# Four-layer graph network on one core: score, attention, adjacency and quantile products queued behind each step's column-tile block

## The chip, the core and the metric

The kernel runs on one core of a Trainium2 chip. The metric is the time of one execution on the device in microseconds (us); the median of the runs shown is compared. A core has engines that run side by side and wait for each other through semaphores: TensorE (PE, matrix products into PSUM; its weight loads are listed apart as PEld), VectorE (DVE), ScalarE (ACT), GpSimd (POOL, idle here) and SyncE (SP, which issues the transfers). Each engine takes its instructions in a fixed order.

## The reference, cut to what matters

`x` is 16 graphs of 1024 nodes with 64 features, `adj` their 0/1 adjacency. Four layers follow each other, each `x = x + f(relu(layernorm(x)), adj)`:

```
layer 0: thin out neighbours by rank (dilation); per node and feature take the 0.25, 0.5 and
         0.75 quantiles over the neighbours, weighted 0.25, 0.5, 0.25; add h; two-layer MLP; mask
layer 1: (adj + I) @ h / rowsum(adj + I)
layer 2: 8 heads: s = exp(gamma0) * q.k/8 + exp(gamma1) * adj; softmax(s) @ v; projection
layer 3: adj @ (h @ W) + bias
```

Layer 0 is the costly one: six order statistics (three quantiles, each between two neighbours in the sorted list) for 1024 nodes, 64 features and 16 graphs ("elements").

## The kernel before, in words

**Two streams.** `picks()` (L760) is layer 0. It makes 16 x 8 x 2 x 6 = 1536 *steps*, 96 an element: element `b`, group `g` of 8 features, half `t` of the nodes (512 columns), order statistic `q`. `layers()` (L1287) is all the rest: it turns every adjacency matrix (`turned`, L1076, during element 0) and then, for an element whose layer 0 is done, runs layers 1, 2 and 3. So layers of element `b` run beside the steps of element `b+1`, and those of the last one run alone after the last step (`alone`). The driver (L1295 to L1299) traces both by due times: a step yields .42, and pieces of layers are traced until their own yields have used that up. The 40.3 units of layers of an element just fill 96 steps.

**A step.** `compare(n)` (L794) makes on DVE three 128x2048 passes: `le` (L800), `wa` (L802), `wb` (L804), in four rotating buffers (`a4`). PE then multiplies them by small stationary matrices 32 columns wide: the *column block*, 16 products at L823, four each of `prep<-wb` and `prep<-wa` and eight of `val<-le`. Each uses one of four column tiles of the 128x128 array (`tile_position`). ACT copies `prep` to `wi` (L830) and `val` to `vs`. One step later `bits` (L835) makes `bit` on DVE and `pz` on PE (L843); two steps later `value` (L846) makes `vs` on DVE (L850), and after a group's sixth statistic the *quantile sums* `agg` (L856, PE, again 32 columns wide, two instructions for each float32 product), which DVE weighs (`w`, L867) in a later step. `prep`, `val` and `pz` share two PSUM buffers (tag `pa`).

Besides, each step advances `group` (L694), which prepares the tables of the step six later: per feature pair a product over the neighbours (`whole`, L716), then `remainder` (L728), `differences` (L737) and `low_part` (L743), all 128x128 on PE, with ACT passes between them; and `background`, the sorting and thinning of the next element, mostly on DVE.

**Layer 2** (L1113) goes through four pairs of heads, and for each through eight chunks of 128 rows (`i`, L1195). A chunk loads its row `ad` (SP, ACT scales it), and for each head `e` makes the *scores* `sp` (L1213: 64 rows of the array, 1024 columns, one PSUM buffer of its own). DVE adds `ad` and takes the minimum (L1226); ACT takes the exponential with a sum (L1235); PE turns the result in eight pieces (`pcols`, L434) that ACT copies to `eT` (L437; two buffers, tag `bt`). The *attention sum* `ao` (L1240) is 32 instructions of 64 columns, one half of the array a head; then ACT's copy `aoT`, the projection `pp` (L1249) and ACT's copy `att`. `residual` (L1135) adds four chunks at a time to `xr` on DVE.

**Layers 1 and 3** use the *adjacency sum* `two` (`weighted`, L1060, L1064): 16 instructions of 64 columns.

**The order of the work.** A scheduler places the instructions of each engine before the run, by readiness in its own model of time, and by priority, which is the order of tracing. `adjoining` (L383) holds a group of PE products together: all but the first are queued behind the first (`issue_after`: an order of issue, no wait for its end) and get high priority. The first stands where the scheduler puts it. It is used for every block named above.

Of the kernel before, what the change touches and what calls it, by code (L numbers as in the profile page):

```python
# [8 lines left out]
F32 = mybir.dt.float32  # L9
# [12 lines left out]
P = 128  # L22
# [3 lines left out]
NQ = 6  # L26
# [12 lines left out]
def tile_preln_adj_stack(  # L39
# [30 lines left out]
    nc = tc.nc  # L70
# [38 lines left out]
    def b4(name, shape=(P, N), dt=F32):  # L109
        return a4(name, shape, dt) if alone else sb.tile(list(shape), dt, tag="b4", bufs=2, name=name)  # L110
# [6 lines left out]
    def small(name, shape, dt=F32, bufs=3):  # L117
        return sb.tile(list(shape), dt, tag="s_" + name, bufs=bufs, name=name)
# [264 lines left out]
    def adjoining(made):  # L383

        first = next(made)
        with tc.issue_after(first.ins), tc.high_priority():
            for _ in made:
                pass


    def norm_relu(xr, h, t2):
# [368 lines left out]
    def picks():  # L760
# [33 lines left out]
        def compare(n):  # L794
            b, g, t, q = steps[n]
            el = els[b]
            hs = slice(t * 512, (t + 1) * 512)
            cum, c1, c0 = tables[b, g, t]
            le = a4("le", (P, 4, 512), HP)
            nc.vector.tensor_tensor(le, cum, bc(el.krow[q][:, None, hs], [P, 4, 512]), OP.is_lt)  # L800
            wa = a4("wa", (P, 4, 512), HP)
            nc.vector.tensor_tensor(wa, le, c0, OP.mult)  # L802
# [13 lines left out]
            nc.tensor.matmul(  # L816
                prep, sel_q[:, q, :], el.kq[:, hs], start=True, stop=False, skip_group_check=True
            )

            def made():  # L820
                for i, (dst, w, r) in enumerate(rounds):
                    for pp in range(4):
                        yield nc.tensor.matmul(  # L823
                            dst[32 * pp : 32 * pp + 32, :], w[pp], r[pp], start=i == 2, stop=i in (1, 3),
                            tile_position=(0, 32 * pp), skip_group_check=True,
                        )

            adjoining(made())
            wi = a2("wi")
            nc.scalar.copy(wi, prep)  # L830
            vs = sb.tile([P, 512], F32, tag="v", bufs=7, name="vs")
            act(vs, val, AF.Copy, scale=1.0 / UP)
            state[n] = [wi, vs]
# [12 lines left out]
        def value(n):  # L846
            b, g, t, q = steps[n]
            el = els[b]
            pz, vs = state.pop(n)
            nc.vector.scalar_tensor_tensor(vs, pz, 80.0, vs, op0=OP.is_equal, op1=OP.mult)  # L850
            vs_of[q] = vs
            if q < NQ - 1:
                return
            agg = pb("agg")
            adjoining(
                nc.tensor.matmul(  # L856
                    agg[32 * (q_ % 4) : 32 * (q_ % 4) + 32, :], sel_t[:, q_ // 4, :], vs_of[q_],
                    start=q_ < 4, stop=q_ > 1, tile_position=(0, 32 * (q_ % 4)),
                    skip_group_check=True,
                )  # L860
                for q_ in range(NQ)
            )
            def weigh(behind):
                hs = slice(t * 512, (t + 1) * 512)
                w = a2("w")
                with tc.issue_after(behind.ins) if behind else ExitStack():
                    nc.vector.tensor_tensor(w, agg, el.coef[:, hs], OP.mult)  # L867
# [192 lines left out]
    def weighted(aT, h):  # L1060

        two = pb("two", (P, P))
        adjoining(
            nc.tensor.matmul(  # L1064
                two[j % 2 * D : j % 2 * D + D, :], h[:, j, :], aT[:, j, :], start=j < 2,
                stop=j >= C - 2, tile_position=(0, j % 2 * D), skip_group_check=True,
            )
            for j in range(C)
        )
        part = small("aoT", [P, P], bufs=2)  # L1070
        nc.scalar.copy(part, two)
        po = pb("po", (P, D))
        nc.tensor.matmul(po, part, ident2, start=True, stop=True)
        return po
# [38 lines left out]
    def layer2(b, xr):  # L1113
# [19 lines left out]
        for pr in range(H // 2):  # L1133
# [50 lines left out]
            for t in range(NH):  # L1184
# [6 lines left out]
                    )  # L1191
                nc.scalar.copy(v[:, 4 * t : 4 * t + 4, :], pv)
            yield 0.5
            for i in range(C):
                if i == C // 2:  # L1195
                    qT = queries(1, False)
                if i % (C // 2) == 0:
                    att = sb.tile([P, C // 2, 2, D], F32, tag="att", bufs=1, name="att")
                    sums = small("sums", [P, C // 2, 2], bufs=2)
                ad = adj_rows(b, i)  # L1200
                act(ad, ad, AF.Copy, scale=gm[:, i, 1:2])
                eTs = []
                ss = [b4("s") for _ in range(2)]
                nms = [None, None]
                cols = slice(i % 4 * P, (i % 4 + 1) * P)
                for e in range(2):
                    if alone and e:
                        sps = [pc_("sp") for _ in range(NH)]
                    else:
                        sp = ps.tile([P, NH, 512], F32, tag="sp", bufs=1, name="sp")  # L1210
                        sps = [sp[:, t, :] for t in range(NH)]
                    adjoining(
                        nc.tensor.matmul(  # L1213
                            sps[t], qT[t * D : (t + 1) * D, t ^ e, cols],
                            kT[t * D : (t + 1) * D, e, :], start=True, stop=True,
                        )
                        for t in range(NH)
                    )
                    if alone and e:
                        parts = [(sps[t], slice(t * 512, (t + 1) * 512)) for t in range(NH)]  # L1220
                    else:
                        parts = [(sp.rearrange("p t k -> p (t k)"), slice(0, N))]
                    for s, hs in parts:

                        nm = small("nm", [P, 1], bufs=6)
                        nc.vector.tensor_tensor_reduce(  # L1226
                            ss[e][:, hs], s, ad[:, hs], -1.0, nms[e] if hs.start else 3.0e38,
                            op0=OP.add, op1=OP.min, accum_out=nm,
                        )
                        nms[e] = nm  # L1230
                while late:
                    residual(*late.pop())
                yield 0.4
                for e in range(2):
                    act(ss[e], ss[e], AF.Exp, bias=nms[e], scale=-1.0, accum_out=sums[:, i % (C // 2), e : e + 1])  # L1235
                    eTs.append(chunk_cols(ss[e], "eT"))
                yield 0.3
                ao = pb("ao", (P, P))
                adjoining(
                    nc.tensor.matmul(  # L1240
                        ao[e * D : (e + 1) * D, :], v[:, j, e * D : (e + 1) * D], eTs[e][:, j, :],
                        start=j == 0, stop=j == C - 1, tile_position=(0, e * D), skip_group_check=True,
                    )
                    for j in range(C) for e in range(2)
                )
                aT = small("aoT", [P, P], bufs=2)
                nc.scalar.copy(aT, ao)
                pp = pb("pp", (P, 2, D))
                nc.tensor.matmul(pp, aT, wproj[:, pr], start=True, stop=True)  # L1249
                nc.scalar.copy(att[:, i % (C // 2)], pp)  # L1250
                if (i + 1) % (C // 2) == 0:
                    late.append((i + 1 - C // 2, att, sums))
                yield 0.3
        residual(*late.pop())

    def layer3(b, xr):
# [80 lines left out]
```

## Time and profile before

| what | us |
|---|---|
| median of 3 runs (lowest, highest) | 12469.6 (12461.9, 12470.75) |
| the profiled execution's own time | 12481.28 |
| its span, first to last instruction | 12479.1 |
| PE busy | 11308.4 (91%) |
| DVE busy | 11269.9 (90%) |
| ACT busy | 10053.6 (81%) |
| first comparison (L800) to the last | 318 to 12053 |
| a middle element (96 steps) | 735 to 758 |
| alone after the last step | 421 |

A line of instruction groups reads: line, engine, operation, what it writes `<-` what it reads, rows*columns of the array for PE, shapes, count | busy time, mean ns of one | idle time of the engine just before them, and what ended it. Ends of PE's instructions are modelled, starts are not: lengths on PE are read from one start to the next. A line of waits reads: who waited `<-` for whom: us in all, times, longest. In a timeline, like instructions in a row are merged (x8), with the engine's idle time before them in brackets.

### The profile page before, as it was taken

The page shows a single profiled execution, that of the slowest core. Times are in us where ns is not written, and L with a number is a line of the kernel's source. Part 1 is how long each engine was busy: PE and PEld are TensorE (multiplying, and loading weights), DVE is VectorE, ACT ScalarE, POOL GpSimd, SP SyncE. Part 2 cuts the span into 40 slices and gives each one's busy share as a digit, 9 for nine tenths or more (in the row PEclk, how much of TensorE's full clock was granted, in tenths as well). Part 3 has the DMA queues.
Part 4 walks back from the last instruction along what each step waited for, and adds up shares of the span by engine and source line. Part 5 has one row for each costly group of instructions (what it writes and reads, how often), then busy time and mean ns, then how long its engine had stood idle before and what let it go on. Part 6 is the DMA issues. An engine that isn't in the chain of part 4 may idle for free. (4 is left out here: it accounts for less than half of the span.)

```text
span 12479.1 us, 216279 instructions
## 1 busy us (share of the span) xinstructions
PE 11308.4 (91%) x85697; PEld 5374.3 (43%) x85697; DVE 11269.9 (90%) x17026; ACT 10053.6 (81%) x17672; POOL 3.3 (0%) x22
## 2 busy tenths in 40 slices
PE   3889989999899998999999998999989999999988
PEld 2334444444444444444444444444444444444445
DVE  8999989899898989989899998999989999887862
ACT  4988878888787887878788887888878888888866
POOL 0000000000000000000000000000000000000000
PEclk6999999999999999999999999999999999999988
DMA  7641121211212122121211212122121212211011
GB/s 238 232 142 56 53 76 59 77 60 54 72 55 80 59 63 65 54 82 57 71 59 60 75 56 74 55 70 68 56 72 55 83 55 60 78 32 56 30 53 57
DMA packets 520552, 908.01 MB, mean 73 GB/s; under 512 B 239728, under 2 KB 274672, under 8 KB 519536
## 3 DMA queue, kind: packets, MB, share of 16 engines
q1 hardware_dynamic: 519536, 894.18, 22.6%
q8 instruction: 672, 11.01, 0.4%
q14 instruction: 344, 2.82, 0.1%
HBM read 683.25 MB, written 206.57 MB: 71 GB/s over the span
## 5 line engine op out<-in xcount | busy, mean ns | idle before, releaser
L802 DVE TENSOR_TENSOR wa<-le,c 128x2048 f16<-128x2048 f16 x1536 | 1871.6, 1218 | 211.1 <-PE prep L823 169.4
L716 PE MATMUL px<-valid,cw 128*128 128x512 fp8e4 x8192 | 1955.5, 380 | 2.0 <-ACT cw L381 2.0
L804 DVE TENSOR_TENSOR wb<-le,c 128x2048 f16<-128x2048 f16 x1536 | 1871.3, 1218 | 0.0
L800 DVE TENSOR_TENSOR le<-cum,krow 128x2048 f16<-128x2048 int16 x1536 | 1868.6, 1217 | 0.6 <-ACT cum L381 0.6
L381 ACT ACTIVATE c<-px,shifts 128x512 f16<-128x512 f32 x2048 | 1432.4, 702 | 153.4 <-PE px L737 82.0
L1226 DVE CUSTOM_DVE_ANT_0 s<-sp,ad 128x1024 f32<-128x1024 f32 (+1 forms) x1024 | 1230.4, 1202 | 332.9 <-PE sp L1213 329.6
L381 ACT ACTIVATE s<-s,nm 128x1024 f32<-128x1024 f32 x1024 | 1189.5, 1162 | 293.7 <-DVE nm L1226 291.4
L716 PEld LDWEIGHTS <-cw 128*128 128x128 f16 x8192 | 800.8, 98 | 1074.2 <-issue 164.4
L1213 PE MATMUL sp<-kT,qT 64*128 64x512 f32 x4096 | 1220.8, 641 | 24.0 <-DVE nm L1226 22.7
L434 PE MATMUL pcols<-identf,s 128*128 128x128 f32 x8192 | 1153.0, 279 | 96.0 <-ACT s L381 48.5
L437 ACT COPY eT<-pcols 128x512 f32<-128x512 f32 x2048 | 1133.8, 605 | 57.9 <-PE pcols L434 54.6
L434 PEld LDWEIGHTS pcols<-identf,s 128*128 128x128 f32 x8192 | 907.6, 141 | 582.0 <-ACT eT L437 212.1
L830 ACT COPY wi<-prep 128x512 f32<-128x512 f32 x1536 | 919.5, 599 | 289.0 <-PE prep L823 266.8
L850 DVE SCALAR_TENSOR_TENSOR vs<-pz,vs 128x512 f32<-128x512 f32 x1536 | 1051.2, 684 | 86.9 <-PE pz L843 83.1
L1240 PE MATMUL ao<-eT,v 128*64 128x128 f32 x16384 | 1080.8, 279 | 28.3 <-ACT eT L437 25.3
L823 PE MATMUL val<-le,tab 128*32 128x512 f16 x12288 | 1063.6, 388 | 29.0 <-DVE vs L850 17.7
L1240 PEld LDWEIGHTS ao<-eT,v 128*64 128x64 f32 x16384 | 918.5, 138 | 289.7 <-ACT eT L437 154.5
L381 ACT ACTIVATE high<-px,shifts 128x512 f16<-128x512 f32 x1024 | 709.2, 693 | 378.6 <-PE px L716 375.3
L381 ACT ACTIVATE vs<-val 128x512 f32<-128x512 f32 x1536 | 953.1, 620 | 56.9 <-PE agg L856 32.5
L838 DVE TENSOR_SCALAR bit<-wi,to 128x512 int32<-128x512 int32 x1536 | 830.8, 541 | 3.8 <-ACT cw L381 2.8
L823 PE MATMUL prep<-wb,sel_w 128*32 128x512 f16 x6144 | 639.2, 395 | 194.6 <-DVE wb L804 191.0
L843 PE MATMUL pz<-bit,nth 128*128 128x512 bf16 x1536 | 615.3, 401 | 192.5 <-DVE bit L838 144.8
(264 smaller groups left out, 18128.8 us busy)
## 6 DMA issues: line engine op xcount, KB each, us to landing
ad<-in_adj_dram SPq DMA_DIRECT2D x768, 512.0 KB
aT<-adjT SPq DMA_DIRECT2D x256, 512.0 KB
adjT<-aT SPq DMA_DIRECT2D x128, 512.0 KB
md<-sm SPq DMA_DIRECT2D x216, 256.0 KB
sb<-md SPq DMA_DIRECT2D x216, 256.0 KB
rem_d<-rem SPq DMA_DIRECT2D x128, 256.0 KB
left_d<-nb SPq DMA_DIRECT2D x128, 256.0 KB
lr<-left_d SPq DMA_DIRECT2D x256, 128.0 KB
```

The source lines that it names most:

```text
L381: nc.scalar.activation(out_, in_, func, **kw)
L434: nc.tensor.transpose(pt[:, c, :], ad[:, (4 * s + c) * P : (4 * s + c + 1) * P], identf)
L437: nc.scalar.copy(aT[:, 4 * s : 4 * s + 4, :], pt)
L716: yield nc.tensor.matmul(px[pp], w[:, j, :], valid[:, j, :], start=False, stop=j == C - 1, skip_group_check=True,)
L800: nc.vector.tensor_tensor(le, cum, bc(el.krow[q][:, None, hs], [P, 4, 512]), OP.is_lt)
L802: nc.vector.tensor_tensor(wa, le, c0, OP.mult)
L804: last = nc.vector.tensor_tensor(wb, le, c1, OP.mult)
L823: yield nc.tensor.matmul(dst[32 * pp : 32 * pp + 32, :], w[pp], r[pp], start=i == 2, stop=i in (1, 3), tile_position=(0, 32 * pp), skip_gr ...
L850: nc.vector.scalar_tensor_tensor(vs, pz, 80.0, vs, op0=OP.is_equal, op1=OP.mult)
L1213: nc.tensor.matmul(sps[t], qT[t * D : (t + 1) * D, t ^ e, cols], kT[t * D : (t + 1) * D, e, :], start=True, stop=True,)
L1226: nc.vector.tensor_tensor_reduce(ss[e][:, hs], s, ad[:, hs], -1.0, nms[e] if hs.start else 3.0e38, op0=OP.add, op1=OP.min, accum_out=nm,)
L1240: nc.tensor.matmul(ao[e * D : (e + 1) * D, :], v[:, j, e * D : (e + 1) * D], eTs[e][:, j, :], start=j == 0, stop=j == C - 1, tile_position ...
```

## The change

`adjoining` returns its last product. A new helper `following` makes a block like `adjoining`, but queues the whole block, its first product too, on PE behind the last product of the *leader*, with priority moved 1000 instructions ahead; its own last product is the next leader. `compare` sets the leader anew at each column block. `following` is used for `agg`, `two`, `sp` and `ao`; in the stretch after the last step (`alone`) it queues nothing.

`agg` and `ao` make their products in the reverse order, so that the first one needs the data that come last. In layer 2 the two heads' scores of a chunk are a step apart (a yield of 0.42 between them), the exponentials and turns have yields of 0.29 each, and `ao` with all that follows it (now `gathered`) is traced an iteration later, behind the second head's scores of the next chunk; the yields of a chunk still add up to 1.0.

```diff
@@ adjoining
         first = next(made)
+        last = first
         with tc.issue_after(first.ins), tc.high_priority():
-            for _ in made:
+            for last in made:
                 pass
+        return last
+
+    leader = []
+
+    def following(made):
+        with ExitStack() as behind:
+            if leader and not alone:
+                behind.enter_context(tc.issue_after(leader[0].ins))
+                behind.enter_context(tc.high_priority(1000))
+            leader[:] = [adjoining(made)]
@@ compare
-            adjoining(made())
+            leader[:] = [adjoining(made())]
@@ value
-            adjoining(
+            following(
...
-                    start=q_ < 4, stop=q_ > 1, tile_position=(0, 32 * (q_ % 4)),
+                    start=q_ > 1, stop=q_ < 4, tile_position=(0, 32 * (q_ % 4)),
...
-                for q_ in range(NQ)
+                for q_ in range(NQ - 1, -1, -1)
@@ weighted
-        adjoining(
+        following(
@@ layer2
+            def gathered(i, eTs, att, sums):
+                ao = pb("ao", (P, P))
+                following(
+                    nc.tensor.matmul(
+                        ao[e * D : (e + 1) * D, :], v[:, j, e * D : (e + 1) * D], eTs[e][:, j, :],
+                        start=j == C - 1, stop=j == 0, tile_position=(0, e * D), skip_group_check=True,
+                    )
+                    for j in range(C - 1, -1, -1) for e in (1, 0)
+                )
+                aT = small("aoT", [P, P], bufs=2)
+                nc.scalar.copy(aT, ao)
+                pp = pb("pp", (P, 2, D))
+                nc.tensor.matmul(pp, aT, wproj[:, pr], start=True, stop=True)
+                nc.scalar.copy(att[:, i % (C // 2)], pp)
+                if (i + 1) % (C // 2) == 0:
+                    late.append((i + 1 - C // 2, att, sums))
+
+            ready = []
             for i in range(C):
...
                 for e in range(2):
+                    s_, nm_ = b4("s"), None
...
-                    adjoining(
+                    following(
...
+                    ss.append((s_, nm_))
+                    if e == 0:
+                        yield 0.42
                 while late:
                     residual(*late.pop())
-                yield 0.4
-                for e in range(2):
-                    act(ss[e], ss[e], AF.Exp, bias=nms[e], scale=-1.0, accum_out=sums[:, i % (C // 2), e : e + 1])
-                    eTs.append(chunk_cols(ss[e], "eT"))
-                yield 0.3
...
-                yield 0.3
+                while ready:
+                    gathered(*ready.pop())
...
+                for e, (s_, nm_) in enumerate(ss):
+                    act(s_, s_, AF.Exp, bias=nm_, scale=-1.0, accum_out=sums[:, i % (C // 2), e : e + 1])
+                    eTs.append(chunk_cols(s_, "eT"))
+                    yield 0.29
+                ready.append((i, eTs, att, sums))
+            gathered(*ready.pop())
         residual(*late.pop())
```

More of the change, by code (lines that the diff above doesn't have):

```diff
@@ L1196, in layer2 @@
                     qT = queries(1, False)
-                if i % (C // 2) == 0:
-                    att = sb.tile([P, C // 2, 2, D], F32, tag="att", bufs=1, name="att")
-                    sums = small("sums", [P, C // 2, 2], bufs=2)
                 ad = adj_rows(b, i)
                 act(ad, ad, AF.Copy, scale=gm[:, i, 1:2])
-                eTs = []
-                ss = [b4("s") for _ in range(2)]
-                nms = [None, None]
+                eTs, ss = [], []
                 cols = slice(i % 4 * P, (i % 4 + 1) * P)
                 for e in range(2):
+                    s_, nm_ = b4("s"), None
                     if alone and e:
@@ L1226, in layer2 @@
                         nc.vector.tensor_tensor_reduce(
-                            ss[e][:, hs], s, ad[:, hs], -1.0, nms[e] if hs.start else 3.0e38,
+                            s_[:, hs], s, ad[:, hs], -1.0, nm_ if hs.start else 3.0e38,
                             op0=OP.add, op1=OP.min, accum_out=nm,
                         )
-                        nms[e] = nm
+                        nm_ = nm
+                    ss.append((s_, nm_))
+                    if e == 0:
+                        yield 0.42
                 while late:
                     residual(*late.pop())
-                yield 0.4
-                for e in range(2):
-                    act(ss[e], ss[e], AF.Exp, bias=nms[e], scale=-1.0, accum_out=sums[:, i % (C // 2), e : e + 1])
-                    eTs.append(chunk_cols(ss[e], "eT"))
-                yield 0.3
[L1238 to L1252, printed above, removed]
-                yield 0.3
+                while ready:
+                    gathered(*ready.pop())
+                if i % (C // 2) == 0:
+                    att = sb.tile([P, C // 2, 2, D], F32, tag="att", bufs=1, name="att")
+                    sums = small("sums", [P, C // 2, 2], bufs=2)
+                for e, (s_, nm_) in enumerate(ss):
[4 more added lines that the diff above has]
+            gathered(*ready.pop())
         residual(*late.pop())
```

## The prediction

> **What bounds the kernel now.** I read four views in this order: the page's busy shares, busy time by stage, the list of waits, and the timeline of TensorE. The page first:
>
> ```profile
> PE 11308.4 (91%) x85697; PEld 5374.3 (43%) x85697; DVE 11269.9 (90%) x17026; ACT 10053.6 (81%) x17672; POOL 3.3 (0%) x22
> ```
>
> TensorE (PE) and VectorE (DVE) are both about nine tenths busy, so an average names no bound. By stage (columns: stretch, its length, then busy time and count of PE, PEld, DVE, ACT, POOL): two middle elements, the last two, and the rest after the last step.
>
> ```profile
> 2442.00:3183.00 741.00, 690.13 (x5301) 325.01 (x5304) 686.06 (x1066) 609.57 (x1072) 0.00 (x0) 0.98 0.21 64
> 3183.00:3941.00 758.00, 697.89 (x5298) 328.64 (x5294) 715.75 (x1046) 613.09 (x1075) 0.00 (x0) 0.98 0.21 65
> ...
> 10647.00:12058.00 1411.00, 1332.80 (x10402) 626.38 (x10400) 1176.51 (x1573) 1169.12 (x2070) 0.00 (x0) 0.99 0.15 48
> 12058.00:12479.00 421.00, 338.79 (x2486) 224.05 (x2486) 125.10 (x280) 230.50 (x445) 0.00 (x0) 0.85 0.18 58
> ```
>
> In a middle element each engine idles 42 to 60 us of 741 or 758: they take turns at being late. In the last two elements there is less background work for DVE, it idles 234 us, and PE only 78: there PE is the bound. Over the ten middle elements (2442 to 9912 us) the same view adds up to 548 us of idle PE and 463 us of idle DVE. What ends DVE's idle time there (who waits, for whom, total us, times, longest):
>
> ```profile
> DVE s L1226 <- PE sp L1213: 101.1, 58, 3.9
> DVE wa L802 <- PE prep L823: 75.9, 85, 2.4
> DVE o L1055 <- PE y L1051: 74.6, 10, 8.0
> DVE w L867 <- PE agg L856: 58.5, 15, 6.0
> DVE vs L850 <- PE pz L843: 30.9, 30, 2.6
> DVE gm L1122 <- PE pg L1120: 23.7, 10, 3.8
> ```
>
> These six are 365 of the 463 us: what DVE waits for last is PE, in four fifths of its idle time. So time taken off PE shortens the run as long as such waits are left, up to some 36 us an element. ACT, at 610 of 750, waits for both.
>
> **What a change of tile size costs on PE.** The timeline of PE alone (start, length, instruction; only starts can be trusted):
>
> ```profile
> 6004.77 0.38 PE L737 MATMUL px<-high,dif 128*128 128x512 f16 x1
> 6004.98 0.38 PE L737 MATMUL px<-low,dif 128*128 128x512 f16 x1
> 6005.29 1.13 PE L1213 MATMUL sp<-kT,qT 64*128 64x512 f32 x4
> ...
> 6011.93 0.60 PE L823 MATMUL val<-le,tab 128*32 128x512 f16 x8
> 6012.46 0.39 PE L737 MATMUL px<-high,dif 128*128 128x512 f16 x1
> ```
>
> Start to start, L737 to L737 is 0.21 us, but L737 to the scores, which use 64 of the 128 rows, is 0.31. Eight val products run four at a time, two passes of 0.21, and what follows starts 0.53 after the first: again 0.10 too much. So **a change between tile sizes costs 0.10 us**, hidden inside "busy", because the ends are modelled. I counted such changes over the trace, taking PE's matmuls in order of start and comparing the rows*columns of neighbours: 8150 in all, 510 in a middle element, 815 us of PE time.
>
> A worse thing happens when two kinds take turns, as at 6000 us:
>
> ```profile
> 5999.76 0.39 PE L823 MATMUL val<-le,tab 128*32 128x512 f16 x1
> 6000.08 0.43 PE L1240 MATMUL ao<-eT,v 128*64 128x128 f32 x2
> 6000.44 0.39 PE L823 MATMUL val<-le,tab 128*32 128x512 f16 x1
> 6000.76 0.43 PE L1240 MATMUL ao<-eT,v 128*64 128x128 f32 x2
> ```
>
> Each round takes 0.68 us, two changes in it, and the four column tiles no longer run side by side: eight rounds last 5.4 us where eight products (0.43) and sixteen ao matmuls (half of the 1.97 that 32 take in one block at 6021.97) would need 1.4.
>
> **The change part by part.** No arithmetic goes or comes; the instructions are the same, in another order.
>
> *Blocks behind the column block (scores L1213, ao L1240, two L1064, agg L856).* Each such block now follows, on PE, the last product of L823 or the block queued there before it. I took the trace's own order, moved every such block to the end of the nearest column block, and counted again: 6345 changes, 1805 fewer. Moved alone, scores give 648, ao 394, two 251, agg 344 (it has the column block's own tile size, so both borders go); the rest comes from moved blocks that meet. 1805 x 0.10 = 180 us of PE. To that comes the lost side-by-side work: 13 of the 512 ao blocks have L823 inside them; of the 4.0 us lost at 6000, 1.6 are the sixteen changes already counted, so 13 x 2.4 = 31. Together about 210 us of PE, 14 us an element for the 15 that have layers beside them.
>
> How much of it reaches the end? In the last two elements PE is the bound: all of it, 28 us. In the 13 others PE and DVE are late in turns; I take seven tenths (between nothing and all; nearest to the row of waits, where 365 of 463 us wait for PE): 13 x 14 x 0.7 = 127. Sum 155 us.
>
> *Reversed order in ao and agg.* The first matmul now needs the last copy of eT or the last vs, so the block starts later but does not stop halfway (ao waited 25 us for eT inside PE, agg 18 in all). Bounds: minus 18 to plus 20 us; nothing is taken, since L716 and L434 can fill PE meanwhile.
>
> *Heads' scores a step apart.* Both heads share one PSUM tile (sp, one buffer), so today the second block waits for DVE's pass over the first (130 us of PE-side idle, weight loads included). A step is 7.7 us and DVE's pass 1.22, so the second will find the tile free. The row `ad` stays one step longer in one of three buffers; ACT waits 91 us for its DMA today, 30 in the middle elements; its issue keeps its place on SP ahead of the scores. Bounds: minus 130 (all of the scores' wait gone) to plus 91 (doubled DMA wait); taken as 0, since other matmuls fill that PE idle time and the loads are issued as early as before.
>
> *The sums an iteration later.* ao(i-1) with its ACT copies (0.28 each) and pp (0.49) now stands behind the second head's scores of i; exp and transposes of i come after. Two eT buffers allow it: transposes and copies of both heads took 5.1 us (6015.08 to 6020.20), ao 2.0, and an iteration is 2.4 steps, 18 us. The residual's DVE work is the same, one iteration later. At the last i of a head pair the order is as before. Taken as 0; if that cover fails, it is a wait of ACT and PE 28 times an element (28 x 15 x 0.2 = 84 us).
>
> *Waits added.* A block that is not ready holds everything chained after it: agg holds scores, scores hold ao, each within one step. Queued behind the whole chain are pz (L843), L728, L737, L716 and the transposes. What that may cost is the second rival.
>
> *After the last step (421 us)* nothing is chained; only the order of tracing differs. Within 20 us either way; 0.
>
> The profiled execution took 12481.3 us around its span of 12479.1; 12481 - 155 = 12326. The median of the runs shown is 12469.6, 12 lower, so the forecast is **12315 us**, 1.2% less.
>
> **A rule that speaks against it.** The Trainium skill, "Perfetto Trace Analysis", section "Identifying the Most-Contended Engine", says that matmul busy time is a bad measure and that PE's headroom is judged by the busy share of weight loads. Here that is PEld's 43%, against DVE's 90%: by the rule PE has room, DVE is the bound, and the order on PE is worth next to nothing, some 12470 us. The waits of DVE above speak for PE. The rule does not see changes of tile size.
>
> **Rivals.** *Nothing gained*: PE's time is freed, but where DVE waits, another wait takes its place, such as o <- y (75 us in ten elements), which the change does not touch. For it: DVE is 93% to 94% busy in middle elements. Against it: the last two elements. 12440 to 12490, say 12465. The case that the scheduler does not place blocks as the words say (an unready block goes later anyway) ends here too.
>
> *Slower: pz pushed back.* With one block of scores behind the column block nothing is lost:
>
> ```profile
> 6026.97 1.13 PE L1213 MATMUL sp<-kT,qT 64*128 64x512 f32 x4
> 6028.19 0.40 PE L843 MATMUL pz<-bit,nth 128*128 128x512 bf16 x1
> ```
>
> pz started as its bit was ready (DVE 6027.59 + 0.54). But in 28 steps an element the second head's scores and ao come together, 1.06 + 1.97 us, and pz would wait 2 us more. DVE's vs needs pz, the next val needs its PSUM slot (tag pa, two buffers, shared with prep and pz), and the blocks chained behind val wait too. Part is covered by DVE's next comparisons (three of 1.22). At 0.5 to 1 us left uncovered: 28 x 15 = 420 steps, 210 to 420 us, so 12525 to 12735; I price it at 0.65 us, 12590. It decides from 155/420 = 0.37 us a step. For it: 83 us of vs <- pz already. Against it: PE's sum of work falls, and the second block is late only in 28 of 96 steps.
>
> *More than forecast*: the waits for sp and agg (160 us in ten elements, 240 in 15) go almost wholly, since these blocks no longer stand behind L716 and transposes. Two thirds of it on top: 12160.
>
> **Chances.** Forecast (12250 to 12420) 0.46; more 0.14; nothing 0.12; slower 0.28. The range holds the first three cases and the lower half of the slow one, to 12600; below it reaches 12120 and leaves out a few hundredths. One measurement of this kernel can tell some 0.2%, 25 us, from no change: faster 0.62 (the first two and a little of the third), same 0.10, slower 0.28.
>
> **What would show it.** Right: some 6300 to 6800 changes of tile size; scores starting 0.53 us after the eight val products do; no L1240 between two L823; waits of DVE for sp and agg down by half; PE busy down by about 200 us with DVE's unchanged. Wrong: vs <- pz, or wa <- prep, grown by over 150 us; column blocks starting later after the end of wb than now (counted over the trace, half of them over 1.4 us); PE idle time grown by more than its busy time fell. If DVE's idle time stays at 46 us a middle element, the gain was not PE's to give.

## The result, and the profile after

The changed kernel takes 12535.7 us (median of 6 runs, 12523.0 to 12541.0) against 12471.0 for the kernel before (6 runs): a ratio of 1.0051, 95% interval 1.0038 to 1.0064. It is slower by half a per cent, where 1.2% faster was forecast. The profiled execution has a span of 12536.1 us, 57 more than before.

The page's busy shares, as shown of before (lines after L395 have moved down by 12 or more: L823 is now L835, L1213 is L1239, L1240 is L1209):

```profile
PE 11159.7 (89%) x85697; PEld 5371.7 (43%) x85697; DVE 11274.3 (90%) x17026; ACT 10044.8 (80%) x17672; POOL 3.3 (0%) x22
```

PE's work did fall, by 149 us, and DVE's stayed. By stage (stretch, length, busy time and count of PE, PEld, DVE, ACT, POOL), two middle elements, the last two, and what comes after:

```profile
2456.00:3194.00 738.00, 677.03 (x5297) 322.99 (x5292) 685.63 (x1065) 609.71 (x1070) 0.00 (x0) 0.99 0.20 64
3194.00:3957.00 763.00, 685.44 (x5291) 326.17 (x5284) 715.89 (x1045) 610.50 (x1073) 0.00 (x0) 0.98 0.20 65
10721.00:12149.00 1428.00, 1333.03 (x10349) 630.43 (x10348) 1172.03 (x1569) 1165.00 (x2063) 0.00 (x0) 0.98 0.15 46
12154.00:12536.00 382.00, 309.29 (x2484) 207.29 (x2476) 122.79 (x278) 227.67 (x445) 0.00 (x0) 0.87 0.20 64
```

A middle pair of elements takes 1501 us instead of 1499 with 26 us less of PE work; the last two take 1428 instead of 1406 (from the first `le` to the last; the 1411 of before in the prediction runs 5 us further); the stretch after the last step takes 382 instead of 421. So the steps lost some 95 us and the end gave back 39. DVE's waits in the ten middle elements (2456 to 9982 us):

```profile
DVE wa L814 <- PE prep L835: 123.6, 95, 5.0
DVE w L879 <- PE agg L868: 90.7, 29, 8.7
DVE o L1067 <- PE y L1063: 80.0, 10, 8.1
DVE vs L862 <- PE pz L855: 42.4, 37, 4.1
DVE m L633 <- PE pm L630: 42.0, 20, 2.3
DVE s L1252 <- PE sp L1239: 23.5, 35, 1.8
```

The wait for the scores went, as forecast (101 to 24 us). Others came in its place: for `prep` 48 more, for `agg` 32 more, and one that was not there at all, `m` for `pm` (the count of neighbours of the next element), 42.

**Where in an element.** The prediction averaged over whole elements. Elements of 735 and of 758 us alternate. Here one of the 758 us kind (element 6, counted from 0) is cut into its first 16 steps, the 64 in the middle and the last 16; before, then after:

```profile
4677.30:4828.60 151.30, 124.01 (x931) 59.25 (x931) 133.34 (x216) 102.38 (x185) 0.00 (x0) 0.92 0.25 79
4828.60:5314.80 486.20, 457.37 (x3429) 210.41 (x3427) 482.10 (x690) 406.59 (x701) 0.00 (x0) 1.00 0.17 54
5314.80:5435.40 120.60, 115.51 (x935) 57.08 (x934) 100.43 (x143) 104.19 (x188) 0.00 (x0) 1.00 0.32 94
```

```profile
4698.20:4851.10 152.90, 125.83 (x894) 59.46 (x895) 132.17 (x215) 101.86 (x183) 0.00 (x0) 0.88 0.25 78
4851.10:5336.10 485.00, 443.25 (x3435) 208.46 (x3433) 482.83 (x692) 405.20 (x701) 0.00 (x0) 0.99 0.17 56
5336.10:5466.20 130.10, 122.30 (x972) 60.32 (x964) 101.82 (x141) 104.76 (x191) 0.00 (x0) 0.99 0.27 81
```

In the middle DVE is busy 482 of 486 us: the change takes 14 us off PE there and the stretch gets 1 us shorter. DVE's idle time, 46 us an element on average, lies nearly all (39 us, mean of elements 1 to 13) in the other 32 steps, where one element gives way to the next, and there the change adds 11 us here.

### The profile page after: what moved, and what is told of

The parts are those of the page before. It is cut to its first block, busy times and chain, and to the rows that moved or that the text cites. A ratio compares the mean times of both kernels' runs of the same rounds, so it can differ in the third digit from the quotient of the medians.

```text
span 12536.1 us, 216254 instructions
## 1 busy us (share of the span) xinstructions
PE 11159.7 (89%) x85697; PEld 5371.7 (43%) x85697; DVE 11274.3 (90%) x17026; ACT 10044.8 (80%) x17672; POOL 3.3 (0%) x22
## 4 chain that ended last, share of the span: by engine, by line
DVE 48%; PE 27%; ACT 12%; issue 6%; DMA 1%; DVEq 0%; ACTq 0%; SPq 0%
DVE wb L816 8%; DVE wa L814 8%; DVE le L812 7%; DVE s L1252 6%; PE px L728 5%; DVE vs L862 4%; DVE bit L850 3%; PE ao L1209 2%; PE sp L1239 2%; PE pcols L446 2%; PE prep L835 2%; PE two L1076 2%; ACT c L381 2%; PE val L835 2%; ACT s L381 2%
## 5 line engine op out<-in xcount | busy, mean ns | idle before, releaser
L728 PE MATMUL px<-valid,cw 128*128 128x512 fp8e4 x8192 | 1983.6, 383 | 2.0 <-ACT cw L381 2.0
L1239 PE MATMUL sp<-kT,qT 64*128 64x512 f32 x4096 | 1255.1, 642 | 13.5 <-DVE nm L1252 9.3
L446 PE MATMUL pcols<-identf,s 128*128 128x128 f32 x8192 | 1190.9, 278 | 64.7 <-ACT s L381 22.2
L449 ACT COPY eT<-pcols 128x512 f32<-128x512 f32 x2048 | 1169.5, 603 | 35.9 <-PE pcols L446 30.3
L1209 PEld LDWEIGHTS ao<-eT,v 128*64 128x64 f32 x16384 | 886.4, 137 | 386.2 <-issue 210.6
L835 PE MATMUL val<-le,tab 128*32 128x512 f16 x12288 | 1018.3, 390 | 33.2 <-DVE vs L862 19.3
L1209 PE MATMUL ao<-eT,v 128*64 128x128 f32 x16384 | 1013.4, 276 | 24.0 <-ACT eT L449 19.5
L835 PE MATMUL prep<-wb,sel_w 128*32 128x512 f16 x6144 | 632.1, 397 | 333.2 <-DVE wb L816 329.1
```

The costliest lines, as they stand in the source:

```text
L446: nc.tensor.transpose(pt[:, c, :], ad[:, (4 * s + c) * P : (4 * s + c + 1) * P], identf)
L728: yield nc.tensor.matmul(px[pp], w[:, j, :], valid[:, j, :], start=False, stop=j == C - 1, skip_group_check=True,)
L835: yield nc.tensor.matmul(dst[32 * pp : 32 * pp + 32, :], w[pp], r[pp], start=i == 2, stop=i in (1, 3), tile_position=(0, 32 * pp), skip_gr ...
L1209: nc.tensor.matmul(ao[e * D : (e + 1) * D, :], v[:, j, e * D : (e + 1) * D], eTs[e][:, j, :], start=j == C - 1, stop=j == 0, tile_position ...
L1239: nc.tensor.matmul(sps[t], qT[t * D : (t + 1) * D, t ^ e, cols], kT[t * D : (t + 1) * D, e, :], start=True, stop=True,)
```

## The experiments

All times are medians; ratios are against the kernel before run on the same chip. To say where a difference lies, each trace is cut at the starts of `le`, as above; the table gives means over elements 1 to 13, then elements 14 and 15 together, then the rest after the last `le`, in us (element 0 varies too, from 938 to 957 up to the first `le` of element 1; before: 952).

| kernel | time | first 16 | middle 64 | last 16 | 14 and 15 | rest |
|---|---|---|---|---|---|---|
| before | 12471 | 139.9 | 479.8 | 126.1 | 1406 | 426 |
| after | 12536 | 141.1 | 479.8 | 130.8 | 1428 | 387 |
| chain_only | 12634 | 140.3 | 488.7 | 127.3 | 1429 | 411 |
| order_only | 12506 | 144.3 | 476.5 | 130.2 | 1406 | 389 |
| order_alone | 12437 | 140.4 | 479.6 | 126.1 | 1409 | 386 |
| tail_early | 12440 | 133.6 | 480.5 | 129.3 | 1429 | 394 |
| order_tail | 12389 | 135.5 | 476.1 | 130.1 | 1406 | 387 |
| order_tail_rev | 12440 | 140.5 | 475.1 | 129.8 | 1410 | 385 |
| tail_fwd | 12485 | 137.9 | 480.9 | 130.3 | 1416 | 393 |
| pe_mid | 12607 | 140.2 | 485.3 | 128.8 | 1441 | 419 |
| pe_end | 12527 | 136.5 | 477.2 | 135.1 | 1426 | 412 |
| pe_less_mid | 12401 | 139.9 | 476.3 | 125.0 | 1385 | 417 |
| pe_less_end | 12335 | 136.3 | 479.4 | 120.4 | 1401 | 418 |

**1. Which half of the change: chaining or order.** `chain_only` has `following` and the reversed products, with layer 2 in the order of before; `order_only` is the reverse:

```diff
 chain_only, against after          order_only, against before
-  if e == 0: yield 0.42             +  scores of e = 0 | yield 0.42 | scores of e = 1
-  while ready: gathered(...)        +  gathered(chunk i-1), exp and turns of chunk i
+  both scores, exp, turns, ao       (adjoining everywhere, products in forward order)
```

> The changed kernel's chaining (following, with agg and ao reversed), but the order of layer 2 of before: both heads' scores in one step, each chunk's attention sum in its own iteration. Theory A (the chaining costs: scores and attention sums can no longer fill PE while it waits for wb): about 12530 to 12580, with the 39 us that the changed kernel gained after the last step not there, prep <- wb waits of PE above 300 us as in the changed kernel (before: 191). Theory B (the new order of layer 2 costs, the chaining itself gives back PE time): 12400 to 12470, prep <- wb near 191.

> The changed kernel's order of layer 2 (heads' scores a step apart, attention sum an iteration later, yields of 0.42 and 0.29), with nothing chained and nothing reversed. Theory A (the chaining costs): 12420 to 12450, which is before less the 39 us after the last step, steps as long as before. Theory B (the new order costs): 12520 or more, the last eight steps of an element at 73 us as in the changed kernel instead of 68.

Measured: chain_only 12634 (ratio 1.0134, 1.0120 to 1.0148), above the range of theory A; order_only 12506 (1.0031, 1.0020 to 1.0043), between its two ranges. Both halves cost, so neither theory holds alone, and they do not add up: chaining (with the reversal) costs 163 on the old order, 30 with the new one. Theory A's sign, PE's waits for wb above 300 us, is not there in chain_only: 247, while PE's wait of the scores for DVE rose from 23 to 99. By the table, chaining costs in the middle (+8.9 an element on the old order); the new order wins there (-3.3) and 37 us after the last step, and loses at both ends of an element. Changes of tile size (products 8 columns wide counted as 32 wide, as in the prediction's count) number 8150 before, 7474 with the new order alone, 7317 with both, 7905 with the chaining alone.

**2. What PE's time is worth, by place.** Two kernels add PE work to the kernel before; two leave out three of the eight products of some sums over the neighbours, so that these neighbours are missing from the output. `<place>` stands for the steps concerned:

```diff
 pe_mid: 24 <= n % 96 < 56; pe_end: not 16 <= n % 96 < 80
-            nc.tensor.matmul(prep, sel_q[:, q, :], ...)
+            for _ in range(3 if <place> else 1): nc.tensor.matmul(prep, sel_q[:, q, :], ...)
 pe_less_mid, pe_less_end
-                for j in range(C):
+                for j in range(3 if <place> else 0, C):
```

> Before, with two further products of 128x128 by 512 columns (0.215 us each, into prep, overwritten by the product that opens prep anyway) in steps 24 to 55 of every element, where DVE is never idle: 16 x 32 x 0.43 = 220 us more work for PE. Theory A1 (PE time is worth nothing where DVE sets the pace): at most 40 us more, 12470 to 12510. Rival, and what the prediction took (seven tenths of PE's time reaches the end wherever it lies): 120 to 220 us more, 12590 to 12690.

> The same two further products, but in the first 16 and the last 16 steps of every element, where DVE waits for PE: again 220 us more work for PE. Theory A1 (PE time counts only where DVE waits for it): 110 to 220 us more, 12580 to 12690, and at least three times what the same work costs in steps 24 to 55. Rival (the place does not matter): the same as in steps 24 to 55 within 40 us.

> Before, with 3 of the 8 products of 0.215 us of each feature pair's sum over the neighbours (L716) left out in the groups prepared in steps 24 to 53 of every element: 16 x 5 x 4 x 3 x 0.215 = 206 us less work for PE, DVE's and ACT's work unchanged, the output without these neighbours. Theory A2 (in the middle of an element DVE is the bound and PE only just keeps up, so that more PE work costs, as two more products a step did with 138 of 220 us, but less PE work returns little): 0 to 60 us less, 12410 to 12470. Rival (PE's time counts there both ways): 100 to 150 us less, 12320 to 12370.

> The same products left out, but in the groups prepared in the last 18 and the first 12 steps of every element, where nearly all of DVE's idle time lies: again 206 us less work for PE. Theory A2: DVE waits for PE there, so more returns than in the middle, 60 to 150 us, 12320 to 12410. Rival (the waits at an element's ends are chains of latency through PE, ACT and DVE and not PE's load; two more products a step cost 59 of 220 us there): at most 60 us less, 12410 to 12470.

| PE work | in the middle | at the ends |
|---|---|---|
| +220 us | +138 (1.0111, 1.0096 to 1.0127) | +59 (1.0051, 1.0038 to 1.0063) |
| -206 us | -70 (0.9943, 0.9930 to 0.9955) | -136 (0.9893, 0.9878 to 0.9908) |

PE's busy time moved by less than the work put in or left out: +131 us in pe_mid, +158 in pe_end, -194 and -196 in the two others.

The first theory (A1) fell with pe_mid: more PE work costs in the middle, as much as PE's busy time grew, and DVE is not "never idle" there. The two kinds of elements differ. The middle stretch of an element of the 735 us kind (element 7), before, in pe_mid and in pe_less_mid:

```profile
5566.90:6041.20 474.30, 445.30 (x3410) 206.38 (x3408) 464.78 (x734) 398.41 (x693) 0.00 (x0) 0.99 0.17 55
5602.70:6086.80 484.10, 455.61 (x3476) 211.19 (x3472) 466.45 (x734) 401.08 (x694) 0.00 (x0) 1.00 0.16 53
5540.50:6008.20 467.70, 435.74 (x3349) 202.38 (x3349) 461.50 (x734) 399.61 (x693) 0.00 (x0) 1.00 0.17 55
```

PE's work counts here both ways: 10 us more make the stretch 10 us longer, and DVE idles 18 us in it instead of 10; 10 us less make it 7 shorter. The middle stretch of element 6, of the 758 us kind, with less PE work:

```profile
4806.10:5291.10 485.00, 443.07 (x3388) 205.26 (x3387) 482.44 (x692) 408.53 (x705) 0.00 (x0) 1.00 0.17 56
```

PE has 14 us less to do, as in the changed kernel, and the stretch is 1 us shorter, DVE still 482: here DVE sets the length. So less PE work in the middle returns most of itself in one kind of element and next to nothing in the other; the table's mean, 3.5 of 480 us, hides this. Of the 70 us saved, 21 lie in elements 14 and 15 (1385 against 1406), where PE is the bound. The expected 0 to 60 for pe_less_mid was a little too low.

The two numbers for the ends cannot be read so directly; pe_end's 59 lies in neither of its two ranges. In pe_end the first 16 steps are 3.4 us shorter than before, though PE has more to do in them: DVE's wait for layer 0's MLP there (o <- y) is 4.3 us an element instead of 7.3, another arrangement of the same work, which other kernels below show too. Without it pe_end would have cost some 44 us more (an estimate, 13 x 3.4). pe_less_end has part of it (5.2 us), so its 136 us may not all be returned PE time.

**3. The end of an element.** The DVE waits over the whole run of order_only show waits that grew with the new order (before: w <- agg 85.0, m <- pm 5.1, o <- y 116.8, rs <- s 22.9):

```profile
DVE w L867 <- PE agg L856: 132.6, 39, 9.6
DVE o L1055 <- PE y L1051: 129.6, 16, 9.3
...
DVE m L621 <- PE pm L618: 64.5, 29, 4.1
DVE rs L1138 <- ACT s L381: 51.8, 40, 1.4
```

And DVE's own timeline in the changed kernel near the end of layer 2 (start, length, instruction, idle before):

```profile
4657.50 0.69 DVE L633 TENSOR_SCALAR m<-pm 128x512 int16<-128x512 f32 x1 [2.33 <-PE pm L630]
...
4660.08 0.69 DVE L1151 TENSOR_TENSOR att<-att,rs 128x512 f32<-128x512 f32 x1
4660.80 0.88 DVE L1155 TENSOR_TENSOR xr<-xr,att 128x256 f32<-128x256 f32 x2
4661.72 0.69 DVE L407 TENSOR_REDUCE mean<-xr 128x8 f32<-128x512 f32 x1
```

The last attention sum, the residual (L1151, L1155) and layer 3's norm (L407) follow at once, just as the next element's positions (`pm`) are made. The kernel before had a yield of 0.3 between the last `ao` and the residual. `tail_early` puts it back:

```diff
                     eTs.append(chunk_cols(s_, "eT"))
-                    yield 0.29
+                    if e == 0 or i < C - 1: yield 0.29
                 ready.append((i, eTs, att, sums))
             gathered(*ready.pop())
+            yield 0.29
         residual(*late.pop())
```

> The changed kernel, but in the last chunk of each head pair the attention sum is traced 0.29 earlier, right behind its own transposes, and the yield stands between it and the residual and layer 3's norm, as in before. Theory B1 (the new order loses at an element's end because the last attention sum, the residual, layer 3's norm and the next element's positions all come due at once): m <- pm and w <- agg waits of DVE fall back towards 0 and 5.6 us an element, 12440 to 12490. If the loss at the end has another cause: 12520 to 12550, waits unchanged.

Measured 12440 (0.9974, 0.9964 to 0.9985): 96 us off the changed kernel, and faster than before by 0.3%. Its DVE waits:

```profile
DVE wa L814 <- PE prep L835: 362.4, 221, 5.0
...
DVE o L1067 <- PE y L1063: 71.1, 16, 8.7
...
DVE w L879 <- PE agg L868: 27.4, 43, 2.6
```

`agg` fell from 134 to 27 us and m <- pm from 62 to 27, as theory B1 wanted, and `y` from 127 to 71, which it had not named. But `prep` rose from 282 to 362, and in the last 16 steps, where the collision is, it took the place of the others (11.5 to 16.9 us an element): they got only 1.5 us shorter. The gain lies in the first 16 steps (141.1 to 133.6), about half of it in o <- y (7.9 to 3.8 us an element); the same holds from order_only to order_tail (144.3 to 135.5, 7.9 to 3.7). So the missing due time is what cost the 96 us, but the collision that B1 blamed is not shown to be the way.

**4. After the last step.**

```diff
+            if alone:
+                (the changed kernel's chunks, adjoining, reversed)
+            else:
                 (the chunks of before)
```

> Before in all steps; the changed kernel's order of layer 2 (attention sum behind the next chunk's scores, its products reversed) only for the head pairs that run after the last step, where nothing is chained in either kernel. If the gain of the changed kernel after the last step (421 us to 382 in the profiles) belongs to that order alone: 12425 to 12445. If it came from the state that the steps leave behind: 12460 to 12475.

Measured 12437 (0.9973, 0.9963 to 0.9983): the gain after the last step belongs to the order, `ao` behind the next chunk's scores, and to nothing in the chain.

**5. Does chaining pay once the end is mended.** `order_tail` is tail_early with `adjoining` everywhere and forward products; `tail_agg_free` leaves `agg` alone unchained, `tail_sp_only` chains the scores alone, `tail_shift` has the yields 0.40 and 0.30.

> The changed kernel's order of layer 2 with the last attention sum of a head pair 0.29 earlier, but nothing chained and nothing reversed. Theory C (the chaining gives nothing: PE's saved changes of tile size become PE's waiting for wb, since DVE is the bound in the middle of an element): 12390 to 12440, no slower than the same kernel chained (12440). Theory D (the chaining pays once the end of the element is mended): 12460 to 12500.

> The kernel with the earlier last attention sum, chained, but the quantile sums agg left free (adjoining, still in reversed order). If agg between the column block and ACT's copy of val costs (ACT vs <- PE agg rose from 32 to 134 us): 12390 to 12425, that wait back near 40 us. If not: 12430 to 12455, or slower by agg's two changes of tile size, 256 x 2 x 0.1 = 51 us, 12490.

> The kernel with the earlier last attention sum, with the scores alone chained behind the column block; attention, adjacency and quantile sums free. If the scores' place is what helps (s <- sp of DVE fell from 330 to 184 us) and the long attention sums behind it are what costs (wa <- prep rose from 169 to 282): 12380 to 12425. If chaining gives nothing whichever block it holds: 12430 to 12450. If the attention sums' place helps: over 12455.

> The kernel with the earlier last attention sum, chained as in the changed kernel, with the yields 0.42 and 0.29 replaced by 0.40 and 0.30 (sum still 1.0). No theory gives this a gain; it measures what a small shift of due times does by itself. If the time hangs on causes named so far: 12425 to 12455. If any new placing of the work moves it by as much as the change did (0.5%): outside 12400 to 12480.

Measured: order_tail **12389** (0.9930, 0.9916 to 0.9944), the fastest of those that do all the work; tail_agg_free 12479 (1.0006, 0.9997 to 1.0015); tail_sp_only 12490 (1.0013, 1.0004 to 1.0022); tail_shift 12442 (0.9973, 0.9962 to 0.9984). Theory C holds for this pair: unchained is no slower, it is 51 us faster. The one small shift of due times tried moves the time by 3 us, so these differences are not what any such shift makes by itself. Chaining only some blocks is worse than chaining all. The waits of PE for wb, tail_early and then order_tail, over the whole run:

```profile
PE prep L835 <- DVE wb L816: 323.5, 315, 4.1
```

```profile
PE prep L823 <- DVE wb L804: 186.9, 177, 4.1
```

Chained, PE stands 137 us longer in front of the column block, which is about all that it had saved (PE busy 11120 against 11243). Of these, 43 us of the wait and 71 of the saving come with the reversal alone (order_tail_rev: 230 and 11173).

**6. Constraint, priority or reversal.**

```diff
 tail_noprio                                         tail_prio
-  behind.enter_context(tc.high_priority(1000))     -  behind.enter_context(tc.issue_after(leader[0].ins))
 order_tail_rev: neither, products reversed; tail_fwd: both, products forward
 order_tail_ao, order_tail_agg: neither, ao or agg alone reversed
```

> The kernel with the earlier last attention sum, chained, but without the priority moved 1000 instructions ahead: a block still has to follow the column block, and is then placed in the order of tracing. If the priority is what costs (blocks go ahead of pz, L716 and the transposes): 12385 to 12415, DVE's wait wa <- prep back near 9 us an element. If the constraint to follow is what costs: 12430 to 12490.

> The same kernel with the priority but without the constraint: a block may go anywhere, and as soon as it is ready. If the priority is what costs: 12430 to 12490. If the constraint is what costs (scores and sums can't fill PE's wait for wb): 12385 to 12415, PE's wait prep <- wb back near 12 us an element from 22.

> The kernel with the new order of layer 2 and the earlier last attention sum, nothing chained, but ao and agg with their products in reverse order as in the changed kernel. If the reversal is what costs in the chained kernel: 12420 to 12450. If it is harmless, as the prediction took it: 12380 to 12400.

> The chained kernel with the earlier last attention sum, ao and agg in forward order. By stretch, chaining cost 4.4 us in the 64 middle steps of an element and 23 us in the last two elements against the same order unchained, while the reversal alone cost 4 us in the first 8 steps of an element. If these are separate costs: 4.4 x 13 + 23 = 80 us above 12389, 12445 to 12490, 64 middle steps at 480 and the last two elements at 1428. If the reversal is the whole cost and the chain is free: 12380 to 12410.

> The unchained kernel with the new order and the earlier last attention sum, with ao alone reversed. If ao's reversal is what cost 51 us: 12425 to 12450, first eight steps of an element at 70 us. If agg's: 12380 to 12400, first eight steps at 66. If each new placing at an element's end lands in one of two arrangements, whatever is reversed: either number, but with the wait o <- y at 3.7 or at 7 us an element, and the time following that wait.

> The same with agg alone reversed. If agg's reversal is what cost: 12425 to 12450, first eight steps at 70 us. If ao's: 12380 to 12400. If both cost alike or neither does: the time goes with the wait o <- y (3.7 or 7 us an element) and not with what is reversed.

The constraint is the queueing behind the leader, the priority the 1000 instructions; a blank was not run.

| | neither | constraint | priority | both |
|---|---|---|---|---|
| forward | 12389 | | | 12485 |
| reversed | 12440 | 12492 | 12467 | 12440 |

ao alone reversed takes 12427 (0.9960, 0.9948 to 0.9973), agg alone 12429 (0.9966, 0.9953 to 0.9978). With the reversal the unchained kernel is slower: by 51 us with both, 38 and 40 with one alone. With it the chain costs nothing on balance, without it 95. What is steady is the place: in the middle 64 steps the pairs that differ in the chaining alone go from 476.1 to 480.9 and from 475.1 to 480.5, constraint alone gives 479.3, priority alone 480.2 (both reversed). So each of the two lengthens an element's middle by 4 to 5 us, by itself, and not by more together. About half of that is idle time of DVE (3.6 us an element with neither; 6.2 with both, 5.4 and 6.3 with one alone), the rest work of DVE that fell into these steps instead of others. It lies mostly in the elements of the 735 us kind (467.6 to 477.0 with both, reversed; the others 483.9 to 484.6). In elements 14 and 15 the chain costs 10 and 19 us. The first 16 steps go either way, for no reason that was found: 140.5 to 133.6 with the reversal, 135.5 to 137.9 without. ao's reversal costs in the middle (478.7), agg's in the first 16 steps (140.4, the wait o <- y at 7 instead of 4 us). The 51 us of both lie there too (135.5 to 140.5). But before and order_only, with nothing reversed, have this wait at 7.3 and 7.9, so the 51 us are the price of that arrangement, and not shown to be the reversal's own.

## Why the prediction was wrong

*Where the forecast and the result part.* The prediction summed 127 us won in 13 elements, 28 in the last two and 0 after the last step. Measured, the 13 elements lose 77 us (an element's first 16 steps +1.2, the middle 64 +0.0, the last 16 +4.7), the last two lose 22, the stretch after the last step wins 39, and the first element 4: together the 57 us between the two profiled spans.

*PE as what DVE waits for last.* The rows were right, the average was not. DVE's 46 us idle an element were spread over all 96 steps in the prediction; they lie in the 32 at its ends. In the 64 middle steps DVE idles 7 of 480, so no more than that could be won. The step that failed is "I take seven tenths ... 13 x 14 x 0.7 = 127": the middle 64 steps gave back nothing, with 9 us less PE work in them (450 to 441). In the last 16 the wait that was to go went, and others took its place: s <- sp fell from 8.3 to 1.2 us an element, while wa <- prep rose from 5.5 to 11.5, w <- agg from 5.4 to 8.4 and m <- pm from 0 to 4.2. The rival "nothing gained" argued so, from DVE's 93 to 94%, and had 0.12. The Trainium skill, "Perfetto Trace Analysis", "Identifying the Most-Contended Engine", judges PE's room by MFU or the busy share of weight loads; the prediction took the second, by which DVE is the bound, and set it aside. For what the change gave back in the middle steps that fits (DVE busy 473 of 480 us). That PE had room there does not: pe_mid's added work cost 138 us.

*1805 fewer changes of tile size, 210 us of PE.* Measured 833 and 149. The counting moved every block right behind the column block. In the trace of the changed kernel, from element 1 to the last `le`, scores stand directly behind a column block or another such block in 874 of 1078 places and ao in 417 of 494, but agg in 99 of 240 and two in 43 of 234; and column blocks are cut into by other products more often than before (429 of 1536 against 364; by 128x128 products 374 against 232). 676 of the 833 come with the order of layer 2, which the prediction took to be worth nothing in itself. The price of a change held. The timeline of PE in the changed kernel:

```profile
5078.48 0.61 PE L835 MATMUL val<-le,tab 128*32 128x512 f16 x8 [0.33 <-DVE vs L862]
5079.03 1.13 PE L1239 MATMUL sp<-kT,qT 64*128 64x512 f32 x4
5080.09 1.97 PE L1209 MATMUL ao<-eT,v 128*64 128x128 f32 x32
5081.98 0.40 PE L855 MATMUL pz<-bit,nth 128*128 128x512 bf16 x1
```

The scores start 0.55 us after the eight val products do, 0.53 forecast: a change between two kinds of tile costs about 0.1 too. That a change of tiling mode drains the engine is what the Trainium skill says in "TensorEngine Tiling (Array Packing)", "Key Properties"; the row agrees, with 0.55 us where two passes of 0.21 would do.

*The last two elements, 28 us.* That PE is the bound there was right: 28 us more PE work (pe_mid) made them 34 us longer, 26 less (pe_less_mid) 21 shorter. But the chain saved no PE time there: PE busy 1329 us before and 1333 after, and the whole took 22 us longer, all of it with the chain (chain_only 1429, order_only 1406).

*The sums an iteration later, taken as 0 ("at the last i of a head pair the order is as before").* This was the dearest step: the order is as before, but the due time between `ao` and the residual had gone, and putting it back was worth 96 us (tail_early), 117 where nothing is chained (order_only to order_tail). It does not undo the loss where it arose: tail_early's last 16 steps still take 129.3 us (before: 126.1), and its first 16 take 6 less than before.

*Reversed order, 0 within 20 us.* 51 us in the unchained kernel, through the arrangement of the first 16 steps (section 6).

*After the last step, 0 within 20.* -39: the order of tracing alone sets it.

*Slower because pz is pushed back.* 12536 lies in the stated range only because of this rival, and it is not shown that the rival is the cause. The burst is real, as the lines above show: pz comes 3 us after the column block. But vs <- pz grew by 23 us in all, not by 210, and wa <- prep by 113 (169 to 282), both under the 150 named as a sign. Two other signs of being wrong came: PE's idle time grew by 206 us, more than its busy time fell, and the column blocks start 1.54 us after wb's end instead of 1.41 (median).

What stays open: why the constraint, or the priority, each lengthen an element's middle by 4 to 5 us, and what pushes `prep` back in the last 16 steps. PE's longer wait for wb goes with the two together, and with the constraint (18.7 us an element against 15.1 with neither, products reversed), but not with the priority alone (14.0), where the scores' wait for DVE is what grew (2.0 to 6.6). And which arrangement the first steps of an element fall into was seen, not explained.

## What to carry to other kernels

Cut a stage into its parts before averaging: time taken off an engine is worth something only in the steps where the others wait for it, and two kinds of iteration can differ in this, as the elements of 735 and 758 us did. When work is moved by an iteration, look at the last iteration: what then comes due at once, and with what it collides. A rule of order that saves an engine's time can make it wait longer elsewhere; try the new order without the rule.

## What the runs showed that was not expected

PE work added in the middle of an element showed in different places. In elements of the 735 us kind the middle itself grew, and DVE idled there (section 2). In pe_mid's element 6, of the 758 us kind, DVE was busy 482.5 of 485.8 us in the middle, no longer than before (486.2), and 6 us came in the last 16 steps (126.4 against 120.6). So one element is not enough to read such a kernel.

The first 16 steps of an element come out in one of two ways in most kernels: with the wait o <- y near 4 us an element (tail_early 3.8, order_tail, order_tail_ao and tail_prio 3.7, pe_end 4.3) or near 7 (before 7.3, the changed kernel and order_only 7.9, order_tail_rev, order_tail_agg and tail_noprio 7.1), and they take 134 to 137 us in the first case, 138 to 144 in the second. Over 13 elements 4 us make some 50, so times that differ by that much here can owe it to this alone.
